# Cross-attention and LoRA-FFN block: exponentials, normalisings and an output product placed at other points of the written order

## The chip, the cores and the metric

The kernel runs on one core of one Trainium2 chip. The metric is device time in microseconds (us), the median over timed runs. A core has a matrix engine (TensorE, "PE" in the profile, its weight loads "PEld"), a vector engine (VectorE, "DVE"), an engine for activations (ScalarE, "ACT"), GpSimd ("POOL") and a queue engine that issues transfers (SyncE, "SP"). Each takes its instructions in the order of its own list and waits for the others by semaphores.

## The reference, cut to what matters

Sixteen sequences of 64 tokens, width 512, go through cross-attention with 32 heads of 128 and then through a feed-forward layer with routed LoRA experts:

```python
q = (layernorm(x) @ Wq); k = ctx @ Wk; v = ctx @ Wv          # 32 heads of 128
score = q @ k^T * scale + position_bias                       # per head, 64 x 64 per sequence
probs = softmax(where(mask, score, -inf));  probs = where(mask, probs, 0)
x = x + (probs @ v) @ Wo
x = x + ffn(layernorm(x))      # base matmul + top-k routed LoRA
```

All 1024 tokens are kept as 8 tiles of 128 tokens.

## The kernel before, in words

Every large product is made of float32 operands split into a high part and a rest (`gh`/`gl`, `oh`/`ol`, `wh`/`wl`, `th`/`tl`): ACT casts the high part (line 70), DVE subtracts it (line 71), and the product is three matmuls (line 259). The projections use a Strassen-Winograd scheme of seven products. Their numbers are 1, 2, 6, 5, 7, 4, 3 in the order in which they are made, with other orders in some places. Products 1, 6, 7 and 4 are added up in one bank of PSUM, called x. After 1, 6 and 7 ACT copies that bank out to a tile `u` before the next of the four may add to it. Products 5 and 3 share the bank y, product 2 has the bank z.

**Keys and values.** Stages of `winograd` make keys (`keys_of`) and values for all heads and store them to DRAM. In the key stages of q = 3 to 6, the 8 tiles of x are loaded (`x_tile`), normalised (`norm`: statistics on DVE, a power on POOL, lines 92 to 98, one ACT pass, line 100), transposed by PE (line 104) and copied to `xT` by ACT (`x_turn`, line 331), two tiles in each stage. Tile t is loaded and normalised after product 1 and turned after product 5. Tile t + 1 is loaded and normalised after product 6 and turned after product 3.

**Attention.** The heads go in 16 pairs. The loop over p has a row for each pair, written as a string:

- `Q` is one of the seven products of the next pair's queries (`Queries`, six matmuls each, copies at line 548, sums at line 559).
- `S` are the scores of a pair's two heads: PE (line 464), bias and scale on DVE (line 467), row maxima on DVE (line 469). It also starts the loads of the next pair's keys and bias.
- `exps_of(1)` is one head's exponentials: eight ACT instructions on 128x64 with their row sums (line 475).
- `soften` normalises one head's probabilities on DVE (lines 481 to 483), transposes them on DVE (`pb`, line 492), copies them on ACT (`pt`, line 494) and crosses quarters by four transfers (line 499).
- `P` is probabilities times values of the pair (`pv_mm`, line 511). It needs both heads' `pt`.
- `O` and `o` are output products for one token tile (`proj_o`: six matmuls and an addition to `acc` on DVE, line 528). `O` works on the newest pair, `o` on the one before it.
- `h` is one `soften` behind the addition of the last output product; `e` is one `exps_of(1)`.

In the first row the string is `QSQQQQQQ`, and both heads' exponentials and both `soften` calls are written into its `S`, before the second product. In the other rows one head's exponentials are in `S`; the other's follow the fifth query product, together with the first head's `soften`. After that product `load_o` also loads the two halves of this row's output weights (`so`) and splits them (`wh`, `wl`).

PE's instructions run as written. The order on DVE, ACT, POOL and SP is set by a planner from priorities, which follow the written order, and from times that it works out in advance. `tc.issue_after(ins)` keeps what is written inside it behind `ins`, but only those instructions that are on the engine of `ins`. `tc.high_priority` moves copies and sums of queries forward.

Of the kernel before, what the change touches and what calls it, by code (L numbers as in the profile page):

```python
# [47 lines left out]
def xattn_ffn_kernel(ctx: ExitStack, tc: tile.TileContext, x, ctxT, wq, wk, wv, wo, fside, mask,  # L48
                     base_wT, base_b, arT, router_b, lora_b, expert_map, out):
    nc = tc.nc  # L50
# [3 lines left out]
    sm = ctx.enter_context(tc.tile_pool(name="sm", bufs=2))  # L54
# [54 lines left out]
    with ExitStack() as actx:  # L109
# [103 lines left out]
        def winograd(mm, n, emit, yzbank=bank, order=ORDER):  # L213

            xb, zb, yb, u, u2, u3 = ({} for _ in range(6))

            def post(i, k):
                if i == 1:
                    u[k] = blk("sn", "u")
                    nc.scalar.copy(u[k], xb[k])  # L220
                elif i == 2:
                    c = blk("ob", "c11")
                    nc.vector.tensor_tensor(c, u[k], zb[k], ALU.add)
                    emit(0, 0, k, c)
                elif i == 6:
                    u2[k] = blk("sn", "u2")
                    nc.scalar.copy(u2[k], xb[k])
                elif i == 7:
                    u3[k] = blk("sn", "u3")
                    nc.scalar.copy(u3[k], xb[k])  # L230
                    c = blk("ob", "c22")
                    nc.vector.tensor_tensor(c, u3[k], yb[k], ALU.add)
                    emit(1, 1, k, c)
                elif i == 4:
                    c = blk("ob", "c21")
                    nc.scalar.copy(c, xb[k])
                    emit(1, 0, k, c)
                elif i == 3:
                    c = blk("ob", "c12")
                    nc.vector.tensor_tensor(c, u2[k], yb[k], ALU.add)  # L240
                    emit(0, 1, k, c)

            for i in order:
                for k in range(n):
                    if i == 1:
                        xb[k] = bank()
                    elif i == 2:
                        zb[k] = yzbank(k)
                    elif i == 5:
                        yb[k] = yzbank(k)  # L250
                    b = xb if i in (1, 6, 7, 4) else zb if i == 2 else yb
                    mm(i, k, b[k], i in (1, 2, 5))
                    post(i, k)
                yield i
# [60 lines left out]
        def x_tile(t):  # L315
            nonlocal xT
            if xT is None:
                xT = ax.tile([P, KC, TOK], F32, tag="ax", name="xT")
            xt = blk("v", "xt")
            with tc.issue_after(stored[-1].ins):  # L320
                nc.sync.dma_start(out=xt, in_=x[t])
            xn = blk("v", "xn")
            norm(sm, [xn], [xt])
            return xn

        def x_turn(t, xn):
            ps = small_bank("pst")
# [2 lines left out]
            dst = xT.rearrange("p k (g a b) -> p g a k b", g=4, a=2)[:, g, a]  # L330
            nc.scalar.copy(dst, ps.rearrange("p (k b) -> p k b", k=KC))

        stored = []

        def emit_k(q):
            def emit(i, j, k, c):
# [10 lines left out]
        with tc.manual_schedule(engines={nc.tensor.engine}):  # L347
# [15 lines left out]
            def keys_of(q, g):  # L363
                xn = {}
                for i in winograd(mm_weights(tc_, g), 2, emit_k(q)):
                    if 3 <= q < 7:
                        t = 2 * (q - 3)
                        if i in (1, 6):
                            xn[i] = x_tile(t + (i == 6))
                        elif i == 5:  # L370
                            x_turn(t, xn[1])
                        elif i == 3:
                            x_turn(t + 1, xn[6])

            stages = (0, "o"), (2, "k"), (3, "k"), (2, "o"), (4, "k"), (5, "k"), (4, "o"), (6, "k"), (6, "o"), (7, "k")
            ops = {}
# [153 lines left out]
            class Queries:  # L530
# [6 lines left out]
                def run(self, g, order):  # L537
                    mm = mm_weights(tx, g)
                    b, s = {}, {}
                    for i in order:  # L540
                        x_ = "x" if i in (1, 6, 7, 4) else "z" if i == 2 else "y"
                        if i in (1, 2, 5):
                            b[x_] = bank()
                        mm(i, 0, b[x_], i in (1, 2, 5))
                        with tc.high_priority(offset=SOON):
                            if i in (1, 6, 7):
                                s[i] = blk("sn", "u")
                                copy = nc.scalar.copy(s[i], b["x"])  # L548
                                if i == 1:
                                    self.first = copy.ins  # L550
                                if i == 7:
                                    self.third = copy.ins
                            if i == 4:
                                self.blocks[1, 0] = blk("ob", "q21")
                                nc.scalar.copy(self.blocks[1, 0], b["x"])
                            for at, key, u, bk in ((2, (0, 0), 1, "z"), (7, (1, 1), 7, "y"), (3, (0, 1), 6, "y")):
                                if i == at:
                                    self.blocks[key] = blk("ob", "q")
                                    add = nc.vector.tensor_tensor(self.blocks[key], s[u], b[bk], ALU.add)  # L559
                                    if i == 7:  # L560
                                        self.last = add.ins
                        yield

                def __call__(self, n=1):
# [18 lines left out]
            nxt = Queries(load_pair(1), ORDER_1)  # L583
            qs(1)
            NP = H // 2
            w, prev, pts, soft, ss, ns, t = None, None, [], [], [], 0, 0
            v = load_v(0)
            pairs = {0: qs, 1: nxt}

# [7 lines left out]
                    soft.append(exps(*ss.pop(0)))  # L597

            for p in range(NP):
                steps = ("QSQQQQQQ" if p == 0 else "SQQQPQQOOQOhOQOOOO" if p + 2 < NP else  # L600
                         "SQQQPQQQQOhSeeOOOOOh" if p + 1 < NP else "PoohOOOOOOO")
                n = 0
                for c in steps:
                    if c == "P":
# [4 lines left out]
                    elif c == "S":  # L609
                        ss += [scores(pairs[ns].head(i), ks[i], bms[i]) for i in range(2)]  # L610
                        ns += 1
                        if ns < NP:
                            ks = [load_k(2 * ns + i) for i in range(2)]
                            bms = [bias_of(2 * ns + i) for i in range(2)]
                        if p == ns - 1:
                            exps_of(1 if p else 2)
                        if p == 0:
                            soften()
                            soften()
                    elif c == "Q":  # L620
                        nxt = pairs[p + 1]
                        nxt(1)
                        n += 1
                        if n == 5 and ss:
                            with tc.issue_after(nxt.third):
                                exps_of(1)
                                soften(nxt.last)
                        if n == 5:
                            with ExitStack() as behind:
                                for e in [e.ins for e in evicted] or [nxt.first]:  # L630
                                    behind.enter_context(tc.issue_after(e))
                                w = load_o(p)
                        if n == 7 and p + 2 < NP:
                            with tc.issue_after(nxt.last):
                                pairs[p + 2] = Queries(load_pair(p + 2), ORDER)
                        if n == 7 and p + 2 == NP:
                            sar = [blk("raw", "sar", F32, (P, 2, NB)) for _ in range(2)]
                            sbw = [blk("raw", "sbw") for _ in range(KC)]
                            slb = blk("g", "slb")
                            nc.sync.dma_start(out=slb, in_=lora_b)  # L640
                            for i in range(2):
                                nc.gpsimd.memset(sar[i][:, :, NAR:NB], 0.0)
                                nc.sync.dma_start(out=sar[i][:, :, 0:NAR], in_=arT[:, 2 * i:2 * i + 2])
                            for kc in range(KC):
                                nc.sync.dma_start(out=sbw[kc], in_=base_wT[:, kc])
                    elif c == "h":
                        soften(added.ins)
                    elif c == "e":
                        behind = list(turned)
                        with tc.issue_after(turned[1].ins):  # L650
                            exps_of(1)
                    elif c == "o":
                        added = proj_o(told, *old)
                        told += 1
                    else:
                        added = proj_o(t, *prev)
                        t += 1
                        if p + 1 == NP and t == 2:
                            w = load_o(p)
# [221 lines left out]
```

## Time and profile before

| | |
|---|---|
| median of three runs | 776.38 us (775.9 to 777.86) |
| the profiled execution | 776.67 us, of it 774.9 us span |
| PE busy | 758.6 us, 98% |
| PEld, DVE, ACT, POOL busy | 629.7, 556.0, 416.4, 123.0 us |
| TensorE clock granted | 0.996 of full |

The profile shows one execution. Busy time is per engine. An engine's idle time is put down to what ended it. The chain of waits leads back from the last instruction to what released each step, and the timeline lists single instructions with the idle time before them. All times in the text are us from the start of the span.

### The profile page before, as it was taken

The numbers are of one execution on the slowest core, as the hardware profiler recorded it, in microseconds if no ns is written. First come the engines' busy times: TensorE is split into PE (matmuls) and PEld (weight loads), VectorE is DVE, ScalarE is ACT, GpSimd is POOL, SyncE is SP. The second block draws the span as 40 slices with busy tenths as digits, with TensorE's granted clock in tenths as the row PEclk, the third lists the DMA queues.
The fourth block names the chain that finished last, engine by engine and source line by source line (L and its number), as shares of the span: only waits on it lengthen the run. The fifth ranks groups of instructions, "written<-read, shape, count | busy, mean of one in ns | idle before, by whom it ended". The sixth has DMA issues, their size and how long they took to land.

```text
span 774.9 us, 16651 instructions
## 1 busy us (share of the span) xinstructions
PE 758.6 (98%) x6186; PEld 629.7 (81%) x6186; DVE 556.0 (72%) x1068; ACT 416.4 (54%) x1165; POOL 123.0 (16%) x143
## 2 busy tenths in 40 slices
PE   8999999999999999969999999999999999999998
PEld 6888887888888888847888888888887888877898
DVE  7995676565665756756778776877777777878875
ACT  5654455445454545556545665566545664575361
POOL 0000000000000513132202222022211221010330
PEclk9999999999999999989999999999999999999999
DMA  7695556464535345465544554446543654462011
GB/s 257 233 293 181 177 168 207 144 193 162 195 125 184 123 144 196 169 199 194 158 153 123 187 184 138 143 154 196 162 145 116 199 179 133 134 205 72 2 50 60
DMA packets 80849, 124.68 MB, mean 161 GB/s; under 512 B 9728, under 2 KB 30976, under 8 KB 80768
## 3 DMA queue, kind: packets, MB, share of 16 engines
q1 hardware_dynamic: 80624, 123.56, 49.3%
q8 instruction: 48, 0.79, 0.4%
q14 instruction: 33, 0.27, 0.1%
q10 hardware_dynamic: 144, 0.06, 0.0%
HBM read 83.74 MB, written 35.65 MB: 154 GB/s over the span
## 4 chain that ended last, share of the span: by engine, by line
PE 91%; DVE 3%; issue 2%; ACT 2%; DMA 1%; SPq 1%; POOL 0%; DVEq 0%; ACTq 0%; POOLq 0%
PE ps L259 73%; PE yz L259 5%; PE ps L727 5%; PE pss L464 4%; PE ps L511 4%; DMA cT<-in_ctxT 1%; ACT p L475 1%; PE pst L104 0%; DVE bs L693 0%; DVE bl L71 0%; PE pt L104 0%; ACT wh L70 0%; DVE acc L528 0%; DVE s L161 0%; DVE ol L71 0%
## 5 line engine op out<-in xcount | busy, mean ns | idle before, releaser
L528 DVE TENSOR_TENSOR acc<-acc,ps 128x512 f32<-128x512 f32 x128 | 87.1, 682 | 26.7 <-PE ps L259 26.0
L475 ACT ACTIVATE p<-p,nm 128x64 f32<-128x64 f32 x256 | 85.7, 338 | 36.4 <-DVE nm L469 36.4
L259 PE MATMUL ps<-wh,oh 128*128 128x512 f32 x256 | 100.0, 391 | 0.0
L259 PE MATMUL ps<-wh,ol 128*128 128x512 f32 x256 | 99.7, 390 | 0.1
L259 PE MATMUL ps<-wl,oh 128*128 128x512 f32 x256 | 99.6, 389 | 0.0
L70 ACT CAST gh<-s 128x512 fp32r<-128x512 f32 (+1 forms) x128 | 64.2, 514 | 60.6 <-PE ps L259 51.8
L71 DVE TENSOR_TENSOR gl<-s,gh 128x512 fp32r<-128x512 f32 (+1 forms) x128 | 70.5, 555 | 32.7 <-ACT gh L70 32.4
L161 POOL TENSOR_TENSOR s<-rq 128x256 f32<-128x256 f32 x32 | 24.6, 768 | 266.6 <-DMA rq<-in_wq 226.9
L71 DVE TENSOR_TENSOR ol<-ps,oh 128x512 fp32r<-128x512 f32 x64 | 39.9, 682 | 34.1 <-ACT oh L70 34.1
L71 DVE TENSOR_TENSOR gl<-raw,gh 128x512 fp32r<-128x512 f32 x48 | 34.6, 722 | 37.0 <-ACT gh L70 25.8
L259 PEld LDWEIGHTS ps<-wh,ol 128*128 128x128 f32 x256 | 48.1, 188 | 10.2 <-DVE ol L71 0.5
L259 PEld LDWEIGHTS ps<-wl,oh 128*128 128x128 f32 x256 | 48.1, 188 | 10.1
L259 PEld LDWEIGHTS ps<-wh,oh 128*128 128x128 f32 x256 | 48.1, 188 | 10.0
L70 ACT CAST gh<-raw 128x512 fp32r<-128x512 f32 x48 | 29.7, 621 | 48.4 <-PE yz L259 29.2
L559 DVE TENSOR_TENSOR q<-u,ps 128x512 f32<-128x512 f32 x48 | 32.9, 686 | 25.7 <-PE ps L259 17.5
L475 ACT ACTIVATION_READ_ACCUMULATOR p<-p,nm 128x1 f32 x256 | 48.4, 189 | 0.0
L455 POOL TENSOR_TENSOR bm<-bm,maskb 128x512 f32<-128x512 f32 x32 | 41.5, 1316 | 28.7 <-DMA bm<-in_fside 28.7
L96 POOL TENSOR_TENSOR rs<-rs,nhalf 128x1 f32<-128x1 f32 x8 | 4.4, 552 | 244.9 <-DVE rs L95 244.9
L70 ACT CAST gh<-rq 128x256 fp32r<-128x256 f32 x48 | 19.5, 406 | 37.3 <-PE ps L259 33.4
L548 ACT COPY u<-ps 128x512 f32<-128x512 f32 x48 | 27.9, 580 | 20.7 <-PE ps L259 11.6
L70 ACT CAST oh<-ps 128x512 fp32r<-128x512 f32 x64 | 33.2, 590 | 10.1 <-PE ps L511 10.1
L511 PEld LDWEIGHTS ps<-pt,v 64*64 64x64 f32 x2048 | 32.0, 135 | 6.2 <-issue 5.9
(259 smaller groups left out, 1989.5 us busy)
## 6 DMA issues: line engine op xcount, KB each, us to landing
kd<-c SPq DMA_DIRECT2D x64, 256.0 KB, 2.2
vd<-c SPq DMA_DIRECT2D x64, 256.0 KB, 2.6
kT<-kd SPq DMA_DIRECT2D x64, 256.0 KB, 3.9
v<-vd SPq DMA_DIRECT2D x64, 256.0 KB, 3.7
raw<-in_wk SPq DMA_DIRECT2D x32, 256.0 KB, 4.0
raw<-in_wv SPq DMA_DIRECT2D x32, 256.0 KB, 4.0
rq<-in_wq SPq DMA_DIRECT2D x32, 256.0 KB, 3.7
bm<-in_fside SPq DMA_DIRECT2D x32, 256.0 KB, 4.2
```

The lines of the kernel that those rows point to most:

```text
L70: first = nc.scalar.copy(hi, src)
L71: return first, (lo_eng or nc.vector).tensor_tensor(lo, src, hi.bitcast(F32), ALU.subtract)
L161: self.eng.tensor_tensor(r, a, b, op)
L259: nc.tensor.matmul(o, lhsT=a, rhs=b, start=first and n == 0, stop=last and n == 2, skip_group_check=True)
L455: nc.gpsimd.tensor_tensor(bm, bm, maskb, ALU.add)
L464: nc.tensor.matmul(ps[a * S:(a + 1) * S, t, :], lhsT=qT[n // 8][:, cq], rhs=kT[m // 8][:, ck], start=True, stop=True)
L475: nc.scalar.activation(p[:, t, :], p[:, t, :], AF.Exp, bias=nm[:, t:t + 1], accum_out=sme[:, t:t + 1])
L511: nc.tensor.matmul(ps[a][d:d + S, t * S:(t + 1) * S], lhsT=v[t // 2][r, t % 2, c], rhs=pt[r, :, t, :], start=True, stop=True)
L528: return nc.vector.tensor_tensor(acc[:, t, :], acc[:, t, :], ps, ALU.add)
L548: copy = nc.scalar.copy(s[i], b["x"])
L559: add = nc.vector.tensor_tensor(self.blocks[key], s[u], b[bk], ALU.add)
L727: nc.tensor.matmul(o, lhsT=a, rhs=b, start=start, stop=stop, skip_group_check=True)
```

## The change

Four places are edited; no instruction is added or taken out.

1. First row: `S` holds one head's exponentials. The other head's are written after the fifth query product, behind the ACT copy of product 7, and the first head's `soften` stands there behind the DVE sum that follows product 7. A new letter `f` at the end of the row is the second head's `soften`, behind the last query sum (product 3). `load_o` of that row moves from the fifth to the seventh query product, and is ordered behind the last sum (DVE) in place of the copy of product 1 (ACT).
2. Last row but one: an `O` moves to between the fifth and the sixth query product, `f` takes the place of `h` behind the seventh, and `S` follows at once.
3. The `soften` of the last pair's second head moves from the last row to the end of the last row but one.
4. `norm` of tile t moves from after product 1 to after product 6, and that of tile t + 1 from after product 6 to after product 7. The ACT pass of each is kept behind the newest ACT copy of that product. Loads and transposes stay where they were.

```diff
                 elif i == 6:
                     u2[k] = blk("sn", "u2")
-                    nc.scalar.copy(u2[k], xb[k])
+                    copied[:] = [nc.scalar.copy(u2[k], xb[k])]
                 elif i == 7:
                     u3[k] = blk("sn", "u3")
-                    nc.scalar.copy(u3[k], xb[k])
+                    copied[:] = [nc.scalar.copy(u3[k], xb[k])]
...
             xn = blk("v", "xn")
-            norm(sm, [xn], [xt])
-            return xn
+            return xn, xt
...
                         if i in (1, 6):
                             xn[i] = x_tile(t + (i == 6))
+                        if i in (6, 7):
+                            with tc.issue_after(copied[-1].ins):
+                                norm(sm, *([a] for a in xn[1 if i == 6 else 6]))
                         elif i == 5:
-                            x_turn(t, xn[1])
+                            x_turn(t, xn[1][0])
                         elif i == 3:
-                            x_turn(t + 1, xn[6])
+                            x_turn(t + 1, xn[6][0])
...
                                     if i == 7:
                                         self.last = add.ins
+                                    if i == 3:
+                                        self.final = add
...
-                steps = ("QSQQQQQQ" if p == 0 else "SQQQPQQOOQOhOQOOOO" if p + 2 < NP else
-                         "SQQQPQQQQOhSeeOOOOOh" if p + 1 < NP else "PoohOOOOOOO")
+                steps = ("QSQQQQQQf" if p == 0 else "SQQQPQQOOQOhOQOOOO" if p + 2 < NP else
+                         "SQQQPQQOQQfSeeOOOOOhh" if p + 1 < NP else "PooOOOOOOO")
...
                         if p == ns - 1:
-                            exps_of(1 if p else 2)
-                        if p == 0:
-                            soften()
-                            soften()
+                            exps_of(1)
...
-                        if n == 5:
+                        if n == (5 if p else 7):
                             with ExitStack() as behind:
-                                for e in [e.ins for e in evicted] or [nxt.first]:
-                                    behind.enter_context(tc.issue_after(e))
+                                for e in evicted or [nxt.final]:
+                                    behind.enter_context(tc.issue_after(e.ins))
                                 w = load_o(p)
...
-                    elif c == "h":
-                        soften(added.ins)
+                    elif c in "hf":
+                        soften((added if c == "h" else nxt.final).ins)
```

More of the change, by code (lines that the diff above doesn't have):

```diff
@@ L331, in x_turn @@
             nc.scalar.copy(dst, ps.rearrange("p (k b) -> p k b", k=KC))
-        stored = []
+        stored, copied = [], []
         def emit_k(q):
@@ L585, in xattn_ffn_kernel @@
             NP = H // 2
-            w, prev, pts, soft, ss, ns, t = None, None, [], [], [], 0, 0
+            w, prev, added, pts, soft, ss, ns, t = None, None, None, [], [], [], 0, 0
             v = load_v(0)
```

## The prediction

> **What bounds the kernel now.** The page first: PE is busy for 98% of the span, no other engine above 72%. The edits add no matmul and take none out, so they can only move the gaps between matmuls. PE's own row in the list of waits says how much there is.
>
> ```profile
> PE 758.6 (98%) x6186; PEld 629.7 (81%) x6186; DVE 556.0 (72%) x1068; ACT 416.4 (54%) x1165; POOL 123.0 (16%) x143
> ...
> PE ps L259 <- ACT u L548: 7.9, 2, 7.2
> ```
>
> Two waits hold 7.9 us, one of them 7.2 us, and both are for the ACT copy of a query bank (L548). The windows place the large one and show a second cost behind it: the granted clock is below 1.00 here and at full rate again from 350.
>
> ```profile
> 330.00:340.00 10.00, 2.93 (x12) 2.08 (x12) 6.96 (x13) 8.30 (x38) 4.40 (x4) 0.90 0.78 266
> 340.00:350.00 10.00, 9.47 (x70) 7.50 (x72) 4.58 (x11) 3.17 (x9) 1.48 (x3) 0.75 0.36 101
> ```
>
> The timelines of PE and ACT there, then ACT one row later:
>
> ```profile
> 332.54 0.39 PE L259 MATMUL ps<-t5l,gh 128*128 128x512 f32 x1
> 340.13 0.80 PE L259 MATMUL ps<-t7h,gh 128*128 128x512 f32 x1 [7.21 <-ACT u L548]
> ```
> ```profile
> 330.60 0.35 ACT L475 ACTIVATE p<-p,nm 128x64 f32<-128x64 f32 x1 [1.96 <-DVE nm L469]
> ...
> 335.92 0.60 ACT L494 COPY pt<-pb 128x512 f32<-128x512 f32 x1
> 336.43 1.13 ACT L70 CAST wh<-so 128x512 fp32r<-128x512 f32 x2
> 337.47 0.40 ACT L70 CAST gh<-rq 128x256 fp32r<-128x256 f32 x1
> 338.98 0.62 ACT L494 COPY pt<-pb 128x512 f32<-128x512 f32 x1 [1.10 <-DVE pb L492]
> 339.50 0.58 ACT L548 COPY u<-ps 128x512 f32<-128x512 f32 x1
> ```
> ```profile
> 352.36 0.33 ACT L475 ACTIVATE p<-p,nm 128x64 f32<-128x64 f32 x1
> 352.60 0.19 ACT L475 ACTIVATION_READ_ACCUMULATOR p<-p,nm 128x1 f32 x1
> 352.69 0.56 ACT L548 COPY u<-ps 128x512 f32<-128x512 f32 x1
> ```
>
> Product 6 was complete at 331.6. Its copy stands in ACT's list behind sixteen exponentials, two `wh` casts, a `gh` cast and both `pt` copies, and ends at 340.08. Product 7 may not add to the bank before. One row later, with one head's exponentials in `S`, the copy stands after the fourth exponential and PE does not wait. The smaller losses, from PE's timeline:
>
> ```profile
> 118.58 0.50 PE L259 MATMUL ps<-t4h,gh 128*128 128x512 f32 x1 [0.33 <-ACT u L230]
> ```
> ```profile
> 348.02 0.69 PE L464 MATMUL pss<-kT,q 128*64 128x64 f32 x16
> 349.10 1.09 PE L464 MATMUL pss<-kT,q 128*64 128x64 f32 x30 [0.40 <-DVE q L559]
> ```
> ```profile
> 685.56 0.39 PE L259 MATMUL ps<-t7l,gh 128*128 128x512 f32 x1
> 686.66 0.50 PE L259 MATMUL ps<-t4h,gh 128*128 128x512 f32 x1 [0.72 <-ACT u L548]
> ...
> 716.76 1.15 PE L511 MATMUL ps<-pt,v 64*64 64x64 f32 x60 [0.49 <-DMA pt<-pb]
> ```
>
> A row shows a matmul as 0.39 us long, but the next one starts 0.227 us after it. A gap therefore costs the distance between starts less 0.227.
>
> **First row: what goes.** The product 7 that was due at 332.54 + 0.227 = 332.77 starts at 340.13: 7.36 us. From 340.13 to 345.19 there are twelve starts in 5.06 us, where twelve take 12 x 0.227 = 2.72: 2.34 us of slow clock. Together 9.70.
>
> Here a rule of the Trainium skill bears, "TensorE: Matmul & The Clock Gate", section "What's actually happening": after an idle window of about 3.4 us the array runs at half rate, and a busy window of that length releases it. The trace agrees for the long gap (0.427 between starts after 7.2 us). After gaps of 0.33 to 0.83 us the starts stay at about 0.23. By the rows, a new wait of under a microsecond costs itself and the 2.34 goes wholly. By the rule, a new wait of 3.4 us or more would cost about 2.3 on top and the first-row gain would be 9.70 - 3.4 - 2.3 = 4.0. I use the rows, because the new wait worked out below is short; the rule belongs to the rivals.
>
> **First row: what is late next.** I count from T, the start of product 7, now 332.77. Product 6 is complete at 331.56 and the exponentials begin at 330.60, 0.333 apart. If its copy stands after the fourth, as one row later, it ends at 332.5 and PE waits for nothing; after the eighth it ends at 333.9 and costs 1.2. I take 0, by the nearer row. The second head's exponentials are behind the copy of product 7, so they cannot come ahead of either copy; 8 x 0.333 = 2.7 us and one query copy of 0.59 end at about T + 5.5, under products 2, 4 and 3.
>
> From the rows of before, with the slow clock taken out (342.47 is T there): the last query sum ends at 349.05, T + 6.6; P starts at 355.0, T + 12.5; its second head is needed 1.03 later, at T + 13.55. The first head's `soften` waits only for the sum after product 7 (about T + 2.9) and has 9 us: nothing. The second head's now starts at T + 6.6. How long this chain takes I read from two rows: reciprocal at 336.05 to the fourth crossing transfer at 341.6, and 366.94 to 372.9 in the next row; each transfer lands 1.9 later. That makes 7.5 and 7.8, with other DVE work between in both. It lands at T + 14.1 to 14.4: PE waits 0.5 to 0.9 in the middle of P. I take 0.8.
>
> Bounds of this wait: 0, if `pb` comes first on DVE. Upward, ahead of the second head's normalising stand, by the written order, two `wl` subtractions (2 x 0.68) and up to seven `gl` of the next queries (7 x 0.42), 4.3 us; the rows already hold about 2 of such work, so 2.5 more, a wait of 3.3. `load_o` moved two products later: its two ACT casts (1.13) lose their edge and fit between exponentials; its loads are on SP ahead of the second head's crossing transfers instead of behind the first's. They wait for buffers that were free at 326 and 331.5, so I take 0; a bias load of the next pair planned ahead of the crossings would cost up to 1. Keys of the next pair are loaded by 313. Their bias (POOL, done at 337.0) is needed at T + 7.4 = 340: nothing. First row: 9.70 - 0.8 = 8.9.
>
> **Last row but one.** The distance 685.56 to 686.66 costs 0.87: product 4 waits for the copy of product 7, with nothing between. An O of six matmuls, 1.36, is put there and covers the copy's 0.59: 0.87 gained. Its operands come from the P before, two products earlier, as in rows p = 1 to 13. But this O used to stand between product 3 and S. Now S meets the last sum at once, as at 348.02. S there took 347.93 to 350.65, 2.72; with outputs ahead of it (374.29 to 376.40) it takes 2.11. Lost: 0.61. Net 0.26; bounds -0.4 (if DVE is late with that sum) and 0.87.
>
> **Last pair's second head.** P at the end takes 714.90 to 717.84, 2.94, against 2.16 at 380.63. The excess of 0.78 is the wait for `pt`. Its `soften` now goes ahead of a P and two output products (2.16 + 2.7 us), so it lands in time. But 1.8 us of DVE (0.2 + 0.2 + 0.69 + 0.71) move into 701 to 707, where DVE was full and evicts the P at 700, and four transfers go past the value loads on SP. Those have until 715. Bounds -0.3 and 0.78; I take 0.5.
>
> **x's passes.** Tile t + 1's ACT pass (0.82) stood ahead of the copy of product 7 in the first of these stages, and PE lost 118.58 - 117.86 - 0.227 = 0.49. With the pass behind the copy that goes: 0.5. In return tile t's pass can no longer run early (at 133.60 for a transpose at 172.27, for instance). It must fit under product 5: twelve matmuls, 2.72, less 0.17 for product 6's end, a copy of 0.59, the pass of 0.82 and 0.2 of semaphores leaves 0.9. One ACT cast of 0.62 in between fits, two don't. DVE and POOL steps (0.69 + 0.17 + 0.15 + 0.55 + 0.16 a tile) have no edge and can still run early. Tile t + 1 has 5.4 us of cover. The loads stay, but their buffers are freed later; the next are a stage away. I take 0 for it; the bounds are 0 and 4 x 0.8.
>
> **Sum.** 8.9 + 0.26 + 0.5 + 0.5 = 10.2. Against the profiled 776.67 us (span 774.9 and 1.8 around it): 766.5. The median of the runs is 0.3 below that execution: **766.2 us**.
>
> **The rivals.**
>
> *P takes over the wait (0.24).* DVE becomes the bound after the last query sum. For it: from there to P it has `wl`, `gl`, `soften`, and 2.8 us for the next scores, about 8 us of work in 7. Against it: only part is ahead of `pb`. Wait of 2 to 4.5, the longest with some slow clock: about 768.5, up to 771.
>
> *The transposes wait for x (0.10).* For it: the cover of 0.9 is thin, and the pass ran up to 39 us early before. Against it: ACT is 54% busy. Two casts in the way at most of the four places: up to 3 us, about 769.
>
> *The copy is not freed (0.05).* The change would not do what it says if the planner put two `wh` casts and a `gh` (1.5) ahead of product 6's copy: T moves by 2.7, 769.
>
> *Slower than before (0.04).* The four crossing transfers of the second head queue on SP behind a load whose buffer is freed only by next-row work, and PE stands idle in the middle of P. To lose all 10.2, with about 2.3 of slow clock, the wait must be 0.8 + 7.9 = 8.7 us, so the transfers must land after 355. Nothing in SP's list of waits is longer than 4.9 in this phase, which speaks against it. Then 777 to 780.
>
> **How the numbers follow.** The forecast's own case has 0.57, with 764.3 at its best (no wait in P, and the 0.83 us wait for `ol` at 357.97 gone too) and 768 at its worst. The range 764.3 to 770.8 takes in that case and most of the first three rivals. A measurement of this kernel can tell about 0.3%, 2.3 us, from no change: only the last rival lies wholly above 774.05, and I leave 0.01 for a mixture of the others. Faster 0.95, same 0.01, slower 0.04.
>
> **What would show it.** Right: no gap between products 5 and 7 near 332.8, granted clock 1.00 from 340 to 350; `u` after about four exponentials; a gap of under 1 us in the first P near 346; no gap at product 4 of the last row but one but one of 0.4 in its S; no wait for `pt` in the last P; none at 118. Wrong: PE waits for `pt` of 3 us or more with a clock below 1.00, waits at `pst` (L104), or a `u` copy behind `wh`.

## The result and the profile after

The changed kernel takes 768.72 us in the median of four runs (767.89 to 768.93). The kernel before, run beside it, takes 776.14 us. The ratio is 0.9899, 95% interval 0.9881 to 0.9916: 7.4 us saved where 10.2 were forecast (766.2 us, range 764.3 to 770.8). The profiled execution took 768.93 us with a span of 767.1 us, 7.8 us less than the span before.

The clock row of the page before has one 8, in the slice from 329 to 349 us:

```profile
PEclk9999999999999999989999999999999999999999
```

From the page after: PE's busy line and the clock row, which has no digit below 9 now. Below them are the same two windows of 10 us as in the prediction (columns: window, its length, then busy us of PE, PEld, DVE, ACT and POOL, the clock granted, the share of DMA and GB/s).

```profile
PE 756.0 (99%) x6186; PEld 627.9 (82%) x6186; DVE 559.8 (73%) x1068; ACT 416.8 (54%) x1165; POOL 124.7 (16%) x143
...
PEclk9999999999999999999999999999999999999999
```
```profile
330.00:340.00 10.00, 9.84 (x97) 7.84 (x95) 6.73 (x12) 8.69 (x38) 4.24 (x4) 1.00 0.67 212
340.00:350.00 10.00, 6.33 (x143) 4.91 (x144) 7.95 (x16) 6.71 (x26) 2.13 (x3) 1.00 0.56 177
```

PE was busy for 2.93 us from 330 to 340; it is busy for 9.84 now, and the clock stays at 1.00. But the next window fell from 9.47 to 6.33. PE's list of waits names what stands there:

```profile
PE ps L259 <- ACT u L550: 3.1, 1, 3.1
PE ps L259 <- DVE gl L71: 1.1, 2, 0.6
```

The place of the old wait, and then the new one, in the timelines of ACT and PE after:

```profile
330.46 0.33 ACT L477 ACTIVATE p<-p,nm 128x64 f32<-128x64 f32 x1
330.70 0.19 ACT L477 ACTIVATION_READ_ACCUMULATOR p<-p,nm 128x1 f32 x1
330.80 0.56 ACT L550 COPY u<-ps 128x512 f32<-128x512 f32 x1
```
```profile
331.39 0.40 PE L259 MATMUL ps<-t5l,gh 128*128 128x512 f32 x1
331.62 0.40 PE L259 MATMUL ps<-t7h,gh 128*128 128x512 f32 x1
...
340.63 0.50 PE L259 MATMUL ps<-t1h,gl 128*128 128x512 f32 x1 [0.56 <-DVE gl L71]
...
343.03 0.39 PE L259 MATMUL ps<-t2l,gh 128*128 128x512 f32 x1
346.53 0.50 PE L259 MATMUL ps<-t6h,gh 128*128 128x512 f32 x1 [3.11 <-ACT u L550]
...
348.12 2.12 PE L513 MATMUL ps<-pt,v 64*64 64x64 f32 x127
350.82 0.27 PE L513 MATMUL ps<-pt,v 64*64 64x64 f32 x1 [0.58 <-issue]
```

Product 6's copy stands after the fourth exponential, and product 7 follows product 5 without a gap: that part is exactly as forecast. Twelve microseconds later PE waits 3.11 us, this time for the copy of product 1 of the *next* row's queries. From ACT's timeline there:

```profile
343.67 0.62 ACT L496 COPY pt<-pb 128x512 f32<-128x512 f32 x1 [2.06 <-DVE pb L494]
...
345.57 0.35 ACT L477 ACTIVATE p<-p,nm 128x64 f32<-128x64 f32 x1 [0.66 <-DVE nm L471]
...
345.92 0.56 ACT L550 COPY u<-ps 128x512 f32<-128x512 f32 x1
```

ACT was idle for 2.06 us before the second head's `pt`, and for 0.66 before an exponential, while the bank it had to copy out was complete soon after 342. It had time; its list had the copy in a late place. DVE's timeline shows what was ahead:

```profile
338.48 0.20 DVE L483 RECIPROCAL rc<-sme 128x8 f32<-128x8 f32 x1
...
342.94 0.70 DVE L494 STREAM_TRANSPOSE pb<-p 128x512 f32<-128x512 f32 x1
...
343.87 0.67 DVE L469 SCALAR_TENSOR_TENSOR p<-pss,bm 128x512 f32<-128x512 f32 x1
...
345.73 0.68 DVE L469 SCALAR_TENSOR_TENSOR p<-pss,bm 128x512 f32<-128x512 f32 x1
```

The second head's `pb` ends at 343.64, and only then follow `pt` (ACT), the next scores' two `p` (DVE, 343.87 and 345.73), and the copy `u` (ACT, 345.92). All of `pb`, `pt`, `p` and `u` take their buffers from one tag, `sn`. The stretches between the starts of PE's stages, up to its first transpose of the feed-forward part, say where the time went. Negative is time saved against the span before:

| stretch | forecast | measured |
|---|---|---|
| up to the first S (x's passes) | -0.5 | -1.16, of it 0.22 before the first transpose of x |
| first S to second S (the old wait and its slow clock) | -9.70 | -9.69 |
| second S to third S (what is late next) | +0.8 | +4.05 |
| third S to S of the last row but one | 0 | +0.31 |
| from there to the P of the last row (the last P but one) | -0.26 | -0.64 |
| from there to the first transpose of the feed-forward part | -0.5 | -0.62 |

The sum is -7.75. In the last rows, PE's timeline after shows the S that follows product 3 at once, and the last P without its wait:

```profile
683.44 0.69 PE L466 MATMUL pss<-kT,q 128*64 128x64 f32 x16
684.29 1.62 PE L466 MATMUL pss<-kT,q 128*64 128x64 f32 x48 [0.17 <-DVE q L561]
...
707.90 2.22 PE L513 MATMUL ps<-pt,v 64*64 64x64 f32 x128
```

### The profile page after: what moved, and what is told of

Same layout as the page of the kernel before. It is cut to its first block, busy times and chain, and to the rows that moved or that the text cites. A ratio compares the mean times of both kernels' runs of the same rounds, so it can differ in the third digit from the quotient of the medians.

```text
span 767.1 us, 16662 instructions
## 1 busy us (share of the span) xinstructions
PE 756.0 (99%) x6186; PEld 627.9 (82%) x6186; DVE 559.8 (73%) x1068; ACT 416.8 (54%) x1165; POOL 124.7 (16%) x143
## 4 chain that ended last, share of the span: by engine, by line
PE 91%; DVE 4%; ACT 2%; issue 1%; DMA 1%; SPq 0%; POOL 0%; DVEq 0%; ACTq 0%; POOLq 0%
PE ps L259 73%; PE yz L259 5%; PE ps L728 5%; PE ps L513 4%; PE pss L466 4%; ACT p L477 1%; DMA cT<-in_ctxT 1%; PE pst L104 0%; DVE gl L71 0%; DVE bs L694 0%; DVE pb L494 0%; PE pt L104 0%; DVE p L485 0%; ACT bh L70 0%; DVE ol L71 0%
```

## The experiments

My theory after the result, called W below: the planner hands out the buffers of one tag in the written order. A copy `u` that shares `sn` with `pb`, `pt` and `p` can't be placed ahead of those that are written before it, even when it is ready and has priority. It would explain both waits. Before, both heads' `pb` and `pt` were written ahead of product 6's `u`; after, the second head's `pb` and `pt` and the next scores' `p` are written ahead of the next row's first `u`. The rivals: too few buffers (S); too much work on DVE behind the last query sum (D); too many exponentials in that place for ACT (E).

### Do the parts add up? (e1, e2, e3)

Three kernels made from the one before: the first row's edits alone, x's passes alone, the last rows alone. e1:

```diff
-                steps = ("QSQQQQQQ" if p == 0 else ...
+                steps = ("QSQQQQQQf" if p == 0 else ...
...
-                            exps_of(1 if p else 2)
-                        if p == 0:
-                            soften()
-                            soften()
+                            exps_of(1)
...
-                        if n == 5:
+                        if n == (5 if p else 7):
```

> The kernel before with the first row's edits alone (second head's exponentials, both soften calls, load_o). If the four parts add up: from the start of the first S to the start of the third S the row is 5.6 us shorter than before (as in the changed kernel), with the 7.2 us wait gone and a 3 us wait for a u copy in front of product 6 of the next row's queries; about 770.6 in all. If the parts disturb each other through the planner's order, the wait in front of product 6 changes by over 1 us.

Measured: 770.72 us, ratio 0.9924 (0.9906 to 0.9942). From the first S to the third the row is 6.54 us shorter, more than the 5.6 of the changed kernel. PE waits 2.55 us for the same copy `u` in front of product 6.

e2 has only the diff's edits to `post`, `x_tile` and `keys_of`:

```diff
+                        if i in (6, 7):
+                            with tc.issue_after(copied[-1].ins):
+                                norm(sm, *([a] for a in xn[1 if i == 6 else 6]))
```

> The kernel before with x's passes alone moved. If they are worth what the stage shows: the first S starts 0.9 to 1.2 us earlier than before, no gap of 0.33 us behind product 7 near 118, and the rest is unchanged: 775.1. My forecast's step had 0.5 us. If the 1.2 us earlier came from elsewhere (start-up), the first S is at most 0.5 earlier.

Measured: 776.25 us, ratio 0.9991 (0.9981 to 1.0). The first S is 1.51 earlier, of it 0.53 before the first transpose of x. Most of that can be scatter of the start: in kernels without this edit that transpose starts from 0.36 earlier to 0.24 later than before. The passes are worth about 1.0. In this profile 1.25 is given back up to the third S: 0.41 up to the second S, where the old wait is 7.69 us in place of 7.21, and 0.84 from there on, where the last matmul of the first P waits 1.41 with no engine named. So the total hardly moves.

e3 has only the strings of the last rows and `f`:

```diff
-                         "SQQQPQQQQOhSeeOOOOOh" if p + 1 < NP else "PoohOOOOOOO")
+                         "SQQQPQQOQQfSeeOOOOOhh" if p + 1 < NP else "PooOOOOOOO")
```

> The kernel before with the last rows' edits alone (O between queries, f, hh). If they add up: 1.3 us shorter from S of the last row but one to the first transpose of the feed-forward part, no wait for pt in the last P and a new wait of about 0.4 us at output products near 700 for ol: 774.9. If the order that the planner finds depends on the other parts, it is under 0.6 us.

Measured: 775.05 us, ratio 0.9991 (0.9979 to 1.0003). From S of the last row but one to the first transpose: 1.32 saved, as in the changed kernel (1.26). What follows: the parts add up, to about 0.9 us. Alone they save 1.0, 6.54 and 1.32 in their stretches, together 0.94, 5.64 and 1.26. The first row differs most, and 0.56 of its 0.9 is the wait for `u` in front of product 6. The totals of e2 and e3 alone could not have shown this; the stretches of the profile did.

### Which resource holds the copy back? (e4, e5, e6)

e4 is the changed kernel, and e5 the kernel before, each with this one edit; e6 is the kernel before with a tenth buffer in `sn`:

```diff
-                                s[i] = blk("sn", "u")
+                                s[i] = blk("ob", "u")
```

> The changed kernel with the query copies u taken from the buffers ob in place of sn (one word; same bytes, ob has eight buffers of which the queries fill about half). Theory W: the planner hands out the buffers of one tag in written order, so the next row's first copy u may not be placed ahead of the second head's pb and pt and the next scores' p, which are written before it. Then the 3.1 us wait in front of product 6 goes, and PE waits in P for the second head's pt in its place, 0.5 to 2.5 us: 766.5 to 768. Theory D: DVE's work behind the last query sum is what the copy waits for, whatever its buffer: the wait stays at 3 us and the time at 768.7.

Measured: 768.92 us, ratio 0.9898 (0.9882 to 0.9915). The wait in front of product 6 is gone: the first P starts at 344.69 and not at 348.12, with the same first S. DVE's list is nearly the same, so W holds here and D falls as an explanation of this wait. The time is not better, since PE then waits in P for the second head's `pt`, where the forecast had put the wait. PE's timeline of e4:

```profile
344.80 1.05 PE L513 MATMUL ps<-pt,v 64*64 64x64 f32 x60
347.45 1.58 PE L513 MATMUL ps<-pt,v 64*64 64x64 f32 x64 [1.60 <-DMA pt<-pb]
348.96 0.79 PE L259 MATMUL ps<-t5h,gh 128*128 128x512 f32 x1
349.55 0.63 PE L259 MATMUL ps<-t5h,gl 128*128 128x512 f32 x1
349.98 0.63 PE L259 MATMUL ps<-t5l,gh 128*128 128x512 f32 x1
```

Behind the wait of 1.60 the full-size starts are 0.43 apart up to 352, against 0.23 at full clock, and the granted clock from 345 to 355 is 0.83. The other part of its time is a wait of 1.41 near 576 that the profile puts down to nothing ("issue"), at a place where all kernels show 0 to 1.7.

> The kernel before with one word changed: the query copies u come from the buffers ob, not sn. Exponentials, soften and all else stay where they were. Theory W (buffers of one tag are handed out in written order): the copy of product 6 was late because both heads' pb and pt are written ahead of it and share its buffers. Then it moves in between the exponentials, and the 7.2 us wait goes without the split: 9.7 us less, less 0.5 to 1.5 of waits in the next row (gl, ol): 767 to 768.5. Theory E (the first row's sixteen exponentials are too much work for ACT in that place, so that they have to be split): the wait stays over 4 us, 772 or more.

Measured: 767.25 us, ratio 0.989 (0.9873 to 0.9906). One word does what the whole change does. ACT's timeline of e5, and the two largest entries in PE's list of waits:

```profile
331.14 0.33 ACT L475 ACTIVATE p<-p,nm 128x64 f32<-128x64 f32 x1
...
331.47 0.56 ACT L548 COPY u<-ps 128x512 f32<-128x512 f32 x1
```
```profile
PE ps L259 <- DVE gl L71: 1.5, 3, 0.6
PE warm L350 <- DVE zero L84: 1.0, 1, 1.0
```

With all sixteen exponentials and both `soften` calls still in `S`, the copy stands after the fourth exponential. E falls: ACT had room for all of it, and the split was not needed to free the copy. The second head's `pt` is also early here, since its `soften` does not wait for the last query sum. From first S to third S this row is 9.28 us shorter than before, against 5.64 in the changed kernel.

> The kernel before with ten buffers sn in place of nine (96 bytes of an unused pad make the room). Theory S (too few buffers: the copy waits for one to come free): the 7.2 us wait shrinks by over 2 us. Theory W (order, not number): 7.2 us as before, 776.5.

Measured: 775.01 us in a single run (the kernel before beside it: 775.61). PE's list of waits of e6:

```profile
PE ps L259 <- ACT u L548: 7.9, 2, 7.2
```

It is the line of the kernel before, to the tenth. One buffer more does nothing to this wait. A larger number was not tried.

The traces fit W in every kernel. In the nine kernels with `u` in `sn`, no `u` of the attention part starts ahead of a `pb`, `pt` or `p` that is written before it. In the four with `u` in `ob` (e4, e5, e8, e9), `u` goes ahead of them in the first two rows. So it is shown that the shared tag makes the copy late. That the planner hands out the buffers of a tag in the written order is the reading that fits all these runs; how the planner works inside is not shown.

### Is it the order behind the last query sum? (e7)

The changed kernel, with the first row's `f` behind the sum after product 7:

```diff
-                        soften((added if c == "h" else nxt.final).ins)
+                        soften(added.ins if c == "h" else nxt.final.ins if p else nxt.last)
```

> The changed kernel with the first row's f behind the sum after product 7 and not behind the last query sum (product 3), so that the second head's normalising may start when its exponentials end, ahead of the two wl subtractions. Both W and the chain that I gave in the forecast say that pb, pt and with them the next row's first copy u come about 2 us earlier: the 3.1 us wait falls to about 1 us or less, 766.5 to 767.5. If it is DVE's total work that counts and not the order, what is put behind takes its place and the wait stays over 2 us.

Measured: 768.68 us, ratio 0.9901 (0.9883 to 0.9919), while its profiled execution took 768.3. The wait for the copy fell from 3.11 to 0.67:

```profile
345.06 0.50 PE L259 MATMUL ps<-t6h,gh 128*128 128x512 f32 x1 [0.67 <-ACT u L550]
```

The second head's `pb` ends at 342.17. Counted from product 7 that is 1.9 us earlier than in the changed kernel, as expected. But from first S to third S only 1.66 is gained (7.30 against 5.64), for the last query sum itself waits for DVE now and holds the second S for 0.66, and the total missed its expectation: the timed runs lie from 766.7 to 769.13, and in the profiled one the middle rows lost 0.89 against the kernel before, 0.39 of it in the unexplained wait near 576 (1.15, before 0.76). So order matters, and part of the gain turns into the next wait.

### The last rows, one edit at a time (e10, e11)

```diff
-                         "SQQQPQQQQOhSeeOOOOOh" if p + 1 < NP else
+                         "SQQQPQQOQQfSeeOOOOOh" if p + 1 < NP else
```

> The kernel before with the O between queries and f alone; the last pair's second soften stays in the last row. If the two edits of the last rows are independent: about 0.65 us gained from S of the last row but one to the P of the last row (0.87 of the copy's wait, less a wait of 0.2 to 0.6 in S), and the 0.49 us wait for pt in the last P still there.

Measured: 775.63 us in a single run (the kernel before beside it: 776.8). 0.66 is gained from S of the last row but one (-0.12) to the P of the last row (-0.78), and the wait for `pt` stays at 0.47. Another 0.32 is gained from there to the last P.

```diff
-                         "SQQQPQQQQOhSeeOOOOOh" if p + 1 < NP else "PoohOOOOOOO")
+                         "SQQQPQQQQOhSeeOOOOOhh" if p + 1 < NP else "PooOOOOOOO")
```

> The kernel before with the last pair's second soften moved up alone. If independent: 0.6 us gained between the P of the last row and the first transpose of the feed-forward part, the 0.72 us wait at product 4 still there, and the wait for ol near 700 no more than 0.2 longer than before.

Measured: 776.96 us in a single run, with 1.70 in the wait near 584. From the P of the last row to the first transpose 1.01 is gained (+1.27 to +0.26), more than the 0.62 in the changed kernel. The 0.72 at product 4 stays. Each edit gains without the other, but the gains do not simply add up: from S of the last row but one to the first transpose they save 0.98 and 1.02 alone, and 1.26 to 1.32 together. In the kernel before, in e3 and in the changed kernel one output product near 700 starts about 0.3 us late on `ol`; in e10 and in e11 it does not. Why is not shown.

### The best version (e8)

The kernel before with `u` in `ob`, x's passes moved and the last rows' edits, without the first row's split.

> The kernel before with u in ob (e5) and the edits to x's passes and to the last rows, without the first row's split. If the parts add up: e5 less 1.2 for x's passes and less 1.3 for the last rows, 765 to 766, and faster than the changed kernel by 3 us.

Measured: 765.57 us, ratio 0.9866 (0.9851 to 0.988), all its runs (764.88 to 766.25) below all those of the changed kernel. It adds up to what e5, e2 and e3 show: 767.25 less 1.0 and 1.3 is about 765. PE's list of waits of e8 begins with:

```profile
PE ps L259 <- DVE gl L71: 1.2, 2, 0.6
...
PE pss L466 <- DVE q L561: 0.7, 2, 0.5
```

Nothing in it is longer than 1.0.

### The slow clock of e4 again (e9)

> The same kernel as e4 once more. In e4 PE waited 1.6 us in the middle of the first P and the next eight starts were 0.427 us apart, at half clock, though after the 3.1 us wait between full-size matmuls of the changed kernel they were not. If the slow stretch belongs to a wait inside P (64x64 matmuls on both sides), it is here again: about eight starts at 0.427 near 350. If it depends on where the wait falls in the time of a clock window, it may be longer, shorter or missing.

Measured: 767.23 us in a single run on another chip (the kernel before beside it: 776.8). The same program waits in the same P, in two pieces of 1.34 and 0.61, and PE goes on at full rate (timeline of e9):

```profile
348.31 1.15 PE L513 MATMUL ps<-pt,v 64*64 64x64 f32 x60 [0.61 <-DMA pt<-pb]
349.39 0.50 PE L259 MATMUL ps<-t5h,gh 128*128 128x512 f32 x1
349.73 0.40 PE L259 MATMUL ps<-t5h,gl 128*128 128x512 f32 x1
```

So the wait at this place need not slow the clock: one execution has the slow stretch and another has not. The waits of the two are not quite alike, 1.60 in one piece against 1.34 and 0.61. But e4's own four executions differ too, with mean granted clocks of 0.998, 0.998, 0.998 and 1.0.

## Why the prediction was right, and where a step failed

**The first row's gain was right to the hundredth.** The wait and its slow clock were to go, 9.70 us together; the second S comes 9.69 us earlier from the first. The choice between the fourth and the eighth exponential, made by the row one later, was right too.

**"What is late next" is the step that failed: 0.8 was put down, 4.05 came.** Three things in it were off.

- The chain of the second head's `soften` was taken from two rows as 5.6 to 6.0 us from its reciprocal to the fourth crossing transfer. It took 7.6 (338.48 to about 346.1), because `wl` and `gl` subtractions stand between its steps: the reciprocal's product with `valid` is finished only 2.7 after the reciprocal began. The upper bound had these, as 2.5 us more; the chosen value did not.
- The wait was looked for only in P. It fell one product earlier, in front of product 6, on the copy `u` of the next row (3.11 us idle, 3.38 with the restart), because this copy stood behind that chain in ACT's list. The prediction asked who waits for `pt`; it did not ask what the planner may not put ahead of it. e4 shows that the place is set by the shared tag: with another tag the copy moves and the wait appears in P, at 1.60, in the middle of the bounds of 0 and 3.3 that were given for it.
- Product 1 of that row waits 0.56 for its `gl` subtraction, 0.84 with the restart, which the prediction did not cost. The 0.83 us wait for `ol` after the first P went, but the last matmul of that P now waits 0.58 with no engine named, and the two cost about the same. S gained 0.24. Together with the 3.38 that is 4.0 of the 4.05.

So the rival "P takes over the wait" had the cause (DVE's list behind the last query sum), though not the place, and nearly the time, 768.5. The rival "the copy is not freed" was wrong for the copy that it meant and right one row later, for another reason than `wh` casts. The original wait was also read wrongly: by e5 it was not the amount of exponentials that made the copy late, but the tag that it shares with what is written ahead of it. The total missed by 2.5 us and not by more because x's passes and the last rows gave 1.2 us more than forecast; that the errors ran against each other is luck.

**x's passes: 0.5 forecast, about 1.0 measured.** The wait at 118 was counted, and it went. A second place was missed: before, at 193.84 ACT held its list for 0.95 us for `nb` and then ran the pass and a transpose's copy ahead of product 7's copy, and PE lost about 0.3 in small pieces between 193 and 198, which a list of gaps does not show. The transposes never waited: the cover of 0.9 us held at all four places.

**The last rows: -0.26 and -0.5 forecast, -0.64 and -0.62 measured.** The 0.87 was right. The loss in S was taken as 0.61 from the second S, with its 0.40 us wait; after, the wait is 0.17, since DVE takes the last query sum at once. In the last P the wait for `pt` went wholly, as forecast, and 0.5 was too little only because part of the 0.78 was held back for new waits. None came: an output product starts about 0.3 us late on `ol` in both kernels, at 706.14 before and at 699.07 after.

**The clock rule.** The rule of the Trainium skill, "TensorE: Matmul & The Clock Gate", section "What's actually happening", was put behind the rows for a wait of under a microsecond. In the profiled execution the 3.11 us wait did not slow the clock (1.00 from 340 to 350), as by the rule. But in e4 the clock fell to 0.83 after only 1.60, which neither the rows of before nor the rule as quoted would give, so "a short wait costs only itself" was too strong.

## What to carry to other kernels

When a ready and urgent instruction stands late in an in-order list, look at what it shares with the instructions ahead of it, the buffer tag first, before moving work away from it: one word in a tag gave what the whole change gave (e5). On top of the rearranged row it gave nothing that the totals show (e4); with the edits at other places and without the rearranged row it gave the best time (e8). When a stall is taken out, follow each list from the last moved instruction on, not only the consumer that comes to mind. Price small edits by the stretch of the profile they touch: e2 and e3 each moved their stretch by over 1 us, and the total told neither from no change.

## What the runs showed of the hardware that was not expected

A wait of 1.60 us inside a P of 64x64 matmuls was followed by about eight full-size starts at 0.43 us in one execution (e4, granted clock 0.83 from 345 to 355); the same program with waits of 1.34 and 0.61 us did not show this (e9, 1.00), nor did the profiled execution of the changed kernel after 3.11 us between full-size matmuls (1.00). Other executions need not agree: a mean clock of 0.998, which e4's profiled execution has, is also found in one of the four timed executions of the changed kernel and in three of the four of e1. The old wait varies as well: where it stays, at 7.1 to 7.7 us (before, e2, e3, e6, e10, e11), 6 to 11 starts behind it are slow and cost 1.4 to 2.4 us. No run here takes P's small matmuls and the moment of the wait apart, so the cause stays open.

A wait that the profile puts down to no engine ("issue") stands near 574 to 586 in eleven of the thirteen profiled executions, from 0.16 to 1.70 us, and always before one of the matmuls 4293 to 4295 of PE's 6186. It is not found in e6 and e8. Its cause is open. Kernels whose totals differ by under 1 us can't be ranked by one profile because of it.
